# Four-layer graph network, layers 1-3: where the transposed adjacency matrix comes from

## The chip, the cores and the metric

The kernel runs on one core of one Trainium2 chip, in float32 throughout. The metric is the device time of one launch in microseconds (us). PE is TensorE, DVE is VectorE, ACT is ScalarE, POOL is GpSimd, and SP is the engine whose queue issues most of the DMA transfers.

## The reference, cut to what matters

There are 64 graphs (B) of 256 nodes (N) with 256 features (D). Each of the four layers is x = layernorm(x + layer(x, adj)). adj is a non-negative weighted matrix of each graph with a random pattern of zeros; the pattern is symmetric but the weights are not, so that the transpose is a different matrix.

- Layer 0 is a recurrence over the 256 nodes (a gated unit whose input is a row of adj's transpose times the states so far).
- Layer 1 is a normalized graph convolution:
```
degree = sum(adj, -1);  dis = where(isinf(degree ** -0.5), 0, degree ** -0.5)
out = relu((adj * dis[:, :, None] * dis[:, None, :]) @ (x @ W.T + b))
```
- Layer 2 is single-head attention with relu'd q, k, v; its scores are multiplied by adj and shifted by -9e15 * (1 - adj), then softmax, then a product with v and an output product.
- Layer 3 is attention with 8 heads of 32 features, masked where adj is not above 0:
```
scores = where(adj > 0, q @ k.T / sqrt(32), -9e15);  attn = softmax(scores);  out = (attn @ v) @ Wo + bo
```

## The kernel before, in words

`_recurrence` does layer 0 for all graphs, one node after another, until about 1527 us of the profiled execution. It leaves its result Hd in device memory. `_layers` (L911) then does layers 1, 2 and 3, and the last function runs only if a flag on the softmax's range is raised.

In `_layers` each graph is an object of class `Graph` (L1021) whose methods each emit one step. The order is written out by hand: `ROUND` (L1245) lists the steps of one round, and the loop at L1256 goes through the rounds. The letter ahead of a step says which graph it works for: in round t, L is graph t+1, A is t, B is t-1, C is t-2 and E is t-3. So five graphs are in work at once, at different stages, and a graph passes through five rounds. Each engine executes its instructions in the order in which this list emits them (the schedule is manual), and waits where an operand isn't there. The last line of `ROUND` holds the step that the change touches, `L.adT`, and `B.norm_a.2`; ahead of it stand `C.s3.1` and `B.f2`; the next round begins with `A.xT.1 B.xT.2 E.o3`.

The steps that matter here:

- `load` (L1029), at the head of round t for graph t+2: three DMAs of 256 KB on SP's queue, x, adj (tile `ad`, in natural layout, 128 rows by two halves) and y, layer 0's result. Within SP's queue they stand in that order; y's load of the first graph waits for layer 0's last store.
- `degrees_a`, `degrees_b` (L1049): row sums of `ad`, and dis by a power on POOL.
- `adT` (L1064): `flipped` (L981) takes a PSUM bank and transposes `ad` with four 128x128 PE instructions (L986, shown as tr_ad). ACT copies the two halves to SBUF with the factor dis (L1068, tile `adT`), and DVE makes layer 3's mask `neg3` from the same bank (L1073): -9e15 where the transposed entry is not above 0, else 0. `adT` is read by the step `g` of layer 1 one round later, `neg3` by the two `s3` steps three rounds later.
- `xT` (L1075): the same four PE transposes for y (tr_x), and one ACT copy (L1078). `xT.1` feeds `t`, `xT.2` feeds layer 2's `qk2`, `xT.3` feeds layer 3's.
- `product` (L991): a 256x256x256 product into a PSUM bank, L996 for all of them; the name of the bank tells which (mm_2f, mm_t, ...; plain mm are the q and k products).
- `s3` (L1170): for four heads, transposed scores on PE (L1180), the mask added on DVE (L1189, tile p), exp on ACT (L1190), and the sum of p's two halves on POOL (L1192, tile p3s).
- `o3` (L1196): sums over p3s by a product with ones on PE (L1206), and the heads' outputs (L1215); `sums(1)` comes last. It reads what `s3.0` and `s3.1` of the round before made.
- `f2` (L1140): the end of layer 2: DVE scales the product mm_2f by the softmax sums (L1144, two halves, tile f) and adds it to y with a relu (L1148).
- `norm_a`, `norm_b`: layernorm's statistics on DVE (L948 to L951), a power on POOL (L952), the shift on DVE (L958) and the scaling on ACT (L960).
- `masks` (L1095): layer 2's shift from `ad` on POOL (L1097).

The PSUM banks `mm` are four, used in turn by every `flipped` and `product`. Tiles of `new` have two buffers unless a number is given, `neg3` has four, `ad` has four, `y` seven.

Of the kernel before, what the change touches and what calls it, by code (L numbers as in the profile page):

```python
# [9 lines left out]
F32 = mybir.dt.float32  # L10
BF16 = mybir.dt.bfloat16
AF = mybir.ActivationFunctionType
ALU = mybir.AluOpType
AX = mybir.AxisListType

NEG = 9000000000000000.0
# [3 lines left out]
P = 128  # L20
# [890 lines left out]
def _layers(tc, ident, Hd, Yd, x, adj, weights, out):  # L911
# [8 lines left out]
    nc = tc.nc  # L920
# [7 lines left out]
    with ExitStack() as ctx:  # L928
# [9 lines left out]
        io = ctx.enter_context(tc.tile_pool(name="l_io", bufs=3))  # L938
# [26 lines left out]
        def bank(name, shape=(P, 2, D)):  # L965
            return ps.tile(list(shape), F32, tag="mm", name=name, bufs=4)

        for c in range(2):
            pt = bank(f"w1_{c}", (P, 2, P))
# [11 lines left out]
        def flipped(src, t):  # L981

            pt = bank(f"tr_{t}")
            for a in range(2):
                for c in range(2):
                    nc.tensor.transpose(  # L986
                        pt[:, a, c * P:(c + 1) * P], src[:, c, a * P:(a + 1) * P], ident
                    )
            return pt
# [12 lines left out]
        def new(tag, t, bufs=2, shape=(P, 2, D)):  # L1002
            return work.tile(list(shape), F32, tag=tag, name=f"{tag}_{t}", bufs=bufs)
# [17 lines left out]
        class Graph:  # L1021
# [7 lines left out]
            def load(self):  # L1029
                b = self.b  # L1030
                self.xin = io.tile([P, 2, D], F32, tag="xin", name=f"xin_{b}")
                nc.sync.dma_start(self.xin, x[b].rearrange("(c p) d -> p c d", p=P))
                self.ad = io.tile([P, 2, N], F32, tag="ad", name=f"ad_{b}", bufs=4)
                nc.sync.dma_start(self.ad, adj[b].rearrange("(c p) m -> p c m", p=P))
                self.y = io.tile([P, 2, D], F32, tag="y", name=f"y_{b}", bufs=7)
                nc.sync.dma_start(self.y, Hd[:, b, :].rearrange("(c p) d -> p c d", p=P))

# [24 lines left out]
                nc.vector.tensor_mul(self.dis, self.dis, self.some)  # L1062

            def adT(self):  # L1064
                pt = flipped(self.ad, f"ad_{self.b}")
                self.adT_sb = new("adT", self.b)
                for c in range(2):
                    nc.scalar.activation(  # L1068
                        self.adT_sb[:, c, :], pt[:, c, :], AF.Copy, scale=self.dis[:, c:c + 1]
                    )  # L1070

                self.neg3 = new("neg3", self.b, 4)
                nc.vector.tensor_scalar(self.neg3, pt, 0.0, -NEG, ALU.is_le, ALU.mult)  # L1073

            def xT(self, l):  # L1075
                pt = flipped(self.y, f"x{l}_{self.b}")
# [179 lines left out]
        for t in range(-1, B + 3):  # L1256
            if 0 <= t + 2 < B:
                graphs[t + 2].load()
            for step in ROUND:
                who, name, *args = step.split(".")  # L1260
                b = t - "LABCE".index(who) + 1
# [213 lines left out]
```

## Time and profile before

| | |
|---|---|
| median of three runs | 3438.73 us (3435.99 to 3442.99) |
| span of the profiled execution | 3437.6 us |
| layer 0, to the last of its PE work | about 1525.7 us |
| layers 1-3, from there | about 1912 us |
| one steady round (tr_ad at 2010.71, then 2039.58) | 28.85 us |
| busy over the span, PE | 3227.2 us (94%) |
| busy over the span, DVE | 2499.7 us (73%) |
| busy over the span, ACT | 1883.7 us (55%) |
| busy over the span, POOL | 1873.5 us (55%) |
| tr_ad on PE (L986), 128x128 | 273 ns each, four in 0.44 us |
| adT on ACT (L1068), 128x256 | 467 ns each |
| neg3 on DVE (L1073), 128x512 | 692 ns |
| layer 2's mask on POOL (L1097), 128x512 | 621 ns |

A row of the profile names the line, the engine, the operation and the tiles (what is written, then what is read), with their shapes. In a timeline, the first number is the start in us from the span's start, the second the time until the end of the group, and the square bracket the idle time ahead of it with the engine and line that ended it. The chain of waits goes back from the last instruction and shows, in order of time, which instruction stood on the path that set the end. The list of waits adds up, for each pair, how long an instruction's engine stood idle for another's result. Busy time of PE is modelled from the starts of pipelined matmuls, so that a busy PE isn't necessarily a PE at its peak.

### The profile page before, as it was taken

How to read it: one execution, taken by the hardware profiler on the slowest of the kernel's cores; microseconds unless marked ns; L12 is line 12 of the kernel's file. 1: busy time of each engine (PE TensorE's matmuls, PEld its weight loads, DVE VectorE, ACT ScalarE, POOL GpSimd, SP SyncE). 2: the span in 40 equal slices, each digit the busy share in tenths (PEclk: the TensorE clock that was granted, in tenths of full speed). 3: DMA queues.
4: the chain of work that ended last, by engine and by line, in shares of the span. 5: the costliest groups of instructions: out<-in, count | busy, mean ns of one | idle time of the engine just before them, and what ended most of it. 6: DMA issues, size and time to landing. Idle time of an engine off the chain costs nothing.

```text
span 3437.6 us, 80347 instructions
## 1 busy us (share of the span) xinstructions
PE 3227.2 (94%) x29350; PEld 2321.8 (68%) x29350; DVE 2499.7 (73%) x7061; ACT 1883.7 (55%) x5010; POOL 1873.5 (55%) x2165
## 2 busy tenths in 40 slices
PE   5699999999889998878999999999999999999997
PEld 3555555555455555547888888888888888888885
DVE  3377777766667777755888888888888887888775
ACT  0155555544445554535666666666666666666664
POOL 2376777766657777733444444444444444444443
PEclk8999999999999999988999999999999999999999
DMA  9856576788777575130111111111111111111100
GB/s 280 245 156 150 159 189 154 169 193 204 194 185 175 148 176 153 58 97 22 47 47 47 47 47 47 47 47 47 47 47 47 47 47 47 47 47 47 47 29 19
DMA packets 389348, 347.88 MB, mean 101 GB/s; under 512 B 107357, under 2 KB 355305, under 8 KB 383721
## 3 DMA queue, kind: packets, MB, share of 16 engines
q1 hardware_dynamic: 371256, 325.82, 35.4%
q10 hardware_dynamic: 17696, 16.91, 1.5%
q8 instruction: 234, 3.83, 0.5%
q14 instruction: 162, 1.32, 0.1%
HBM read 224.01 MB, written 99.61 MB: 94 GB/s over the span
## 4 chain that ended last, share of the span: by engine, by line
PE 73%; DMA 7%; DVE 7%; POOL 4%; issue 3%; ACT 3%; SPq 2%; ACTq 0%; DVEq 0%; POOLq 0%
PE mm L996 13%; PE rc L604 5%; PE s L1180 4%; PE rc L596 4%; PE mm_2f L996 3%; PE mm_3v L996 3%; PE mm_t L996 3%; PE mm_3f L996 3%; PE mm_2v L996 3%; PE mm_g L996 3%; PE mm_2s L996 3%; PE mm_2w L996 3%; PE o L1215 3%; PE late L520 3%; DVE ACC L629 3%
## 5 line engine op out<-in xcount | busy, mean ns | idle before, releaser
L629 DVE SCALAR_TENSOR_TENSOR ACC<-keep,S,ACC 128x128 f32<-128x128 f32 x1712 | 504.0, 344 | 186.4 <-ACT hs L647 171.5
L1192 POOL TENSOR_TENSOR p3s<-p 128x256 f32<-128x256 f32 x512 | 387.2, 788 | 369.1 <-ACT p L1190 369.0
L996 PE MATMUL mm<-xT,weights 128*128 128x256 f32 x2048 | 483.9, 385 | 3.2 <-ACT xT L1078 3.2
L996 PEld LDWEIGHTS mm<-xT,weights 128*128 128x128 f32 x2048 | 386.4, 191 | 80.6 <-issue 25.5
L1189 DVE TENSOR_TENSOR p<-s,neg 128x512 f32<-128x512 f32 x512 | 317.5, 682 | 118.2 <-PE s L1180 118.2
L666 POOL TENSOR_TENSOR ACC<-ACC,far 128x384 f32<-128x384 f32 (+1 forms) x313 | 372.7, 1191 | 24.5
L596 PE MATMUL rc<-WxT,xqT 128*64 128x256 f32 x2048 | 324.6, 396 | 3.7 <-ACT rc L837 1.2
L662 POOL TENSOR_TENSOR far<-hs,S 128x384 f32<-128x384 f32 (+1 forms) x313 | 304.9, 974 | 4.7
L960 ACT ACTIVATE y<-y,shift,rstd 128x256 f32<-128x256 f32 x512 | 273.4, 599 | 47.4 <-DVE shift L958 43.4
L1190 ACT ACTIVATE p<-p 128x512 f32<-128x512 f32 x512 | 295.2, 628 | 2.1 <-DVE p L1189 1.6
L803 POOL TENSOR_TENSOR ready<-ACC,dinv 128x128 f32<-128x128 f32 x255 | 102.3, 401 | 335.3 <-DVE ACC L629 335.2
L1103 ACT ACTIVATE qk<-mm,weights 128x256 f32<-128x256 f32 x256 | 107.5, 471 | 268.0 <-PE mm L996 268.0
L1092 POOL TENSOR_TENSOR y<-y,g 128x512 f32<-128x512 f32 x64 | 81.1, 1267 | 267.7 <-issue 267.7
L1229 DVE RECIPROCAL rT<-o 128x256 f32<-128x256 f32 x128 | 223.8, 1748 | 0.3 <-PE o L1206 0.2
L948 DVE BATCH_NORM_STATS2 st<-y 128x6 f32<-128x256 f32 x512 | 209.0, 408 | 13.5 <-POOL y L1092 12.7
L952 POOL TENSOR_TENSOR rstd<-rstd,mhalf 128x2 f32<-128x2 f32 x256 | 173.9, 698 | 82.1 <-DVE rstd L951 80.3
L613 ACT COPY xpT<-xpT_ps 128x128 f32<-128x128 f32 x256 | 68.3, 267 | 259.3 <-PE xpT_ps L611 259.3
L604 PE MATMUL rc<-WhT,xpT 128*64 128x128 f32 x2048 | 170.2, 288 | 29.1 <-ACT xpT L613 28.9
L1057 POOL TENSOR_TENSOR dis<-dis,mhalf 128x2 f32<-128x2 f32 x64 | 44.9, 702 | 276.0 <-DVE dis L1056 265.0
L604 PEld LDWEIGHTS rc<-WhT,xpT 128*64 128x64 f32 x2048 | 107.8, 137 | 120.2 <-ACT xpT L613 84.0
L1155 ACT ACTIVATE qk<-mm,weights 128x256 f32<-128x256 f32 x256 | 107.5, 471 | 118.4 <-PE mm L996 118.4
L596 PE MATMUL z_ps<-WxT,xqT 128*64 128x128 f32 x2048 | 169.7, 287 | 0.0
(162 smaller groups left out, 7418.4 us busy)
## 6 DMA issues: line engine op xcount, KB each, us to landing
xX<-in_x_dram ACTq DMA_DIRECT2D x16, 1024.0 KB
Us<-xu SPq DMA_DIRECT2D x64, 256.0 KB
xq<-in_x_dram SPq DMA_DIRECT2D x64, 256.0 KB
ACC<-Us SPq DMA_DIRECT2D x32, 512.0 KB
Es<-eu SPq DMA_DIRECT2D x64, 256.0 KB
early_sb<-Es SPq DMA_DIRECT2D x32, 512.0 KB
xin<-in_x_dram SPq DMA_DIRECT2D x64, 256.0 KB
ad<-in_adj_dram SPq DMA_DIRECT2D x64, 256.0 KB
```

What stands on the lines that cost most here:

```text
L596: nc.tensor.matmul(G[o * B:(o + 1) * B], xqT[a, i // 2][:, i % 2, kc, h * B:(h + 1) * B], WxT[:, kc, o, gates], start=False, stop=False, s ...
L604: nc.tensor.matmul(G[o * B:(o + 1) * B], hT[:, kc * B:(kc + 1) * B], WhT[:, kc, o, g], start=False, stop=(kc == 1), skip_group_check=True,)
L629: nc.vector.scalar_tensor_tensor(acc[:, 0, :], keep[:, j % 2, :], s, acc[:, 0, :], ALU.mult, ALU.add)
L662: nc.gpsimd.tensor_mul(tmp[:, 0:count, :], hs.unsqueeze(1).to_broadcast(shape), s.unsqueeze(2).to_broadcast(shape),)
L666: nc.gpsimd.tensor_add(acc, acc, tmp[:, 0:count, :])
L948: nc.vector.bn_stats(st, y[:, c, :])
L960: nc.scalar.activation(y[:, c, :], y[:, c, :], AF.Identity, bias=shift[:, c:c + 1], scale=rstd[:, c:c + 1],)
L996: nc.tensor.matmul(pm[:, c, :], lhsT[:, k, c * P:(c + 1) * P], rhs[:, k, :], start=(k == 0), stop=(k == 1),)
L1189: nc.vector.tensor_add(p, s_ps[i], self.neg3)
L1190: nc.scalar.activation(p, p, AF.Exp, scale=ISQ)
L1192: nc.gpsimd.tensor_add(both, p[:, 0, :], p[:, 1, :])
L1229: nc.vector.reciprocal(rT, o_ps[:, 1, :])
```

## The change

`load` gets a second load of adj, tile `az`, in eight DMAs between those of `ad` and y: each takes 32 columns of adj, all 256 rows, as eight blocks of 32x32, so that a row of a block is a run of 128 bytes. After them, partition j*32 + r of `az` holds row r of the blocks whose transposes belong on partitions j*32 to j*32 + 31 of adj's transpose, one block beside the other. `adT` turns all of these blocks by one DVE instruction, a transpose within 32x32 blocks over 128x512 elements, into a new SBUF tile `adTr`. PE's four transposes, and the PSUM bank that they took, are gone. ACT's scaled copies read `adTr` instead of the bank, and the mask `neg3` is made from `adTr` by POOL instead of DVE. The order in `ROUND` is the same. The steps `xT` and `pT2` still transpose on PE.

```diff
@@ load
                 nc.sync.dma_start(self.ad, adj[b].rearrange("(c p) m -> p c m", p=P))
+                self.az = io.tile([P, 2, 8, 32], F32, tag="az", name=f"az_{b}", bufs=3)
+                for j in range(4):
+                    for a in range(2):
+                        at = a * P + j * 32
+                        nc.sync.dma_start(
+                            self.az[j * 32:(j + 1) * 32, a],
+                            adj[b, :, at:at + 32].rearrange("(i r) c -> r i c", r=32),
+                        )
                 self.y = io.tile([P, 2, D], F32, tag="y", name=f"y_{b}", bufs=7)
@@ adT
-                pt = flipped(self.ad, f"ad_{self.b}")
+
+                turned = new("adTr", self.b)
+                nc.vector.transpose(
+                    turned.rearrange("p a m -> p (a m)"), self.az.rearrange("p a i c -> p (a i c)")
+                )
                 self.adT_sb = new("adT", self.b)
                 for c in range(2):
                     nc.scalar.activation(
-                        self.adT_sb[:, c, :], pt[:, c, :], AF.Copy, scale=self.dis[:, c:c + 1]
+                        self.adT_sb[:, c, :], turned[:, c, :], AF.Copy, scale=self.dis[:, c:c + 1]
                     )
 
                 self.neg3 = new("neg3", self.b, 4)
-                nc.vector.tensor_scalar(self.neg3, pt, 0.0, -NEG, ALU.is_le, ALU.mult)
+                nc.gpsimd.tensor_scalar(self.neg3, turned, 0.0, -NEG, ALU.is_le, ALU.mult)
```

Eight lines are added in `load` and three in `adT`, so that the lines of the changed kernel after `load` stand 8 to 12 higher.

## The prediction

> **What bounds the kernel now.** I read first the page's head and the busy time by stretch of the span, to see which part the change can touch.
>
> ```profile
> span 3437.6 us, 80347 instructions
> 1900.00:2300.00 400.00, 400.00 (x2693) 323.75 (x2693) 321.89 (x791) 254.76 (x554) 189.87 (x235) 1.00 0.14 45
> ```
>
> The second line gives busy us of PE, PE's weight loads, DVE, ACT and POOL, then clock and DMA share. From about 1530 us on, layers 1-3 run round after round, and PE is never idle. It looks as if every PE microsecond removed were a microsecond won. So I went to the chain of waits of one round (start, us, what), where the removed transposes stand:
>
> ```profile
> 2008.79 1.92 PE mm_2f L996 x8
> 2010.71 0.44 PE tr_ad L986 x4
> 2011.15 0.87 PE tr_x L986 x8
> 2012.02 0.57 PE o L1206 x8
> 2012.59 1.73 PE o L1215 x32
> 2014.32 0.92 PE o L1206 x8
> 2015.24 1.92 PE mm L996 x8
> ```
>
> tr_ad is 0.44 us of a 28.84 us round (tr_ad recurs at 2039.58). But the two groups of eight L1206 matmuls, the same work, take 0.57 and 0.92 us. The list of waits (total us, times, longest, over 2000 to 3200) names the rest:
>
> ```profile
> PEld o L1206 <- POOL p3s L1192: 14.5, 42, 0.6
> DVE p L1189 <- PE s L1180: 73.6, 42, 2.1
> DVE neg L1073 <- ACT adT L1068: 9.3, 42, 0.9
> ```
>
> 14.5/42 = 0.35 us a round: the second L1206 group waits for POOL's last p3s. Here PE is not the bound: the chain s (PE) to p (DVE) to exp (ACT) to p3s (POOL) is. Next, the DVE and ACT timelines of that stretch (start, duration):
>
> ```profile
> 2008.80 2.48 DVE L1189 TENSOR_TENSOR p<-s,neg 128x512 f32<-128x512 f32 x4 [1.74 <-PE s L1180]
> 2011.21 0.86 DVE L1144 SCALAR_TENSOR_TENSOR f<-mm_2f,sums,weights 128x256 f32<-128x256 f32 x2
> 2012.10 1.16 DVE L1148 SCALAR_TENSOR_TENSOR y<-f,y 128x512 f32<-128x512 f32 x1
> 2013.46 0.69 DVE L1073 TENSOR_SCALAR neg<-tr_ad 128x512 f32<-128x512 f32 x1 [0.20 <-ACT adT L1068]
> 2014.07 0.42 DVE L948 BATCH_NORM_STATS2 st<-y 128x6 f32<-128x256 f32 x1
> ```
> ```profile
> 2010.52 2.19 ACT L1190 ACTIVATE p<-p 128x512 f32<-128x512 f32 x4
> 2012.61 0.82 ACT L1068 ACTIVATE adT<-tr_ad,dis 128x256 f32<-128x256 f32 x2
> 2013.32 1.07 ACT L1078 COPY xT<-tr_x 128x512 f32<-128x512 f32 x2
> ```
> ```profile
> 2011.29 3.28 POOL L1192 TENSOR_TENSOR p3s<-p 128x256 f32<-128x256 f32 x4 [2.93 <-ACT p L1190]
> 2015.51 0.70 POOL L952 TENSOR_TENSOR rstd<-rstd,mhalf 128x2 f32<-128x2 f32 x1 [0.95 <-DVE rstd L951]
> 2015.17 1.99 PE L996 MATMUL mm<-xT,weights 128*128 128x256 f32 x8
> ```
>
> POOL's last p3s ends at 2014.57. ACT's second xT copy, which the mm at 2015.17 reads, ends at 2014.39: 0.78 us early. ACT could start adT at 2012.61 because tr_ad was done at 2011.15. DVE runs without a gap from 2008.80, when PE's scores release it, to the end of y at 2013.26.
>
> **What the Trainium skill says.**
> - "VectorE: DVE Perf Modes", The three transpose paths: DVE transposes 32x32 blocks only, and a 128x128 bf16 tile takes 311 ns. No transpose on DVE is in this trace.
> - "ScalarE: Activation LUTs", What ACT_TABLE_LOAD costs: an ACTIVATE takes 186 ns + 0.833 ns an element, 93 ns more for each [128,1] operand, and consecutive ones overlap by 93 ns. The trace agrees for SBUF sources (p, 512 elements: 613 by the page, 628 here; L960, 256 and two operands: 586, 599 here) and is quicker from PSUM (adT: 493, 467 here).
> - "SBUF — State Buffer", Who interferes with whom: a DVE instruction with two SBUF inputs or in a two-port mode and one of GpSimd exclude each other. Here y (L1148, two SBUF inputs) takes 1.16 us beside p3s, and 0.69 us at 1582.98 with POOL idle.
>
> **Removed.** Four transposes (0.44 us of PE) and a PSUM bank use per graph, 64 x 0.44 = 28 us of PE work. In the steady round they lie between the scores' end and the second L1206 group, which waits for POOL in any case: with tr_ad gone that wait is 0.35 + 0.44 us. I take a gain of nothing; the most it could be is 28 us. DVE's neg3, 0.69 us, goes too. It delays only norm_a, whose rstd POOL takes at 2015.51; nothing on PE waits for that.
>
> **Moved to POOL.** neg3 from SBUF: the same form at L1097 takes 0.62 us. It stands after the fourth p3s (2014.57) and ahead of rstd (2015.51), in POOL's 0.95 us of idle time, and layer 3 reads it rounds later: nothing. If it came late, rstd, then C.norm_b.2, would slip; these have more time if PE's round gets longer.
>
> **Added on DVE: the transpose, and its place.** In program order it stands behind both f and y, and ACT's adT now waits for it, while both xT copies are queued behind adT on ACT. That turns an idle cover into a path: PE scores, DVE p, f, y, transpose, ACT adT, xT, PE mm. The duration isn't in the trace. By the page's 311 ns for 128 elements at 0.96 GHz, 171 cycles are fixed, so 512 elements give (512 + 171)/0.96 = 711 ns: an estimate. Lower bound 0.68 us (the SBUF-read reduction of 128x512, L1052, 676 ns). Upper bound 1.3 us, if it needs two cycles an element (1.24 us) or must wait for p3s as y does (y's 1.16 - 0.69 = 0.47 us on top gives 1.2). I take 0.71. Its eight DMA waits become queue instructions of the kind seen ahead of L1148, 21 ns each; that one ran 1.3 us before its instruction started, so they hide behind y.
>
> **adT from SBUF.** One pointer operand, SBUF source: L1017 shows 502 ns, against 467 from PSUM. Two with 0.1 us overlap: 0.79 us until xT starts, instead of 0.71.
>
> The sum for a round, on the old clock: DVE instructions overlap by 0.08, so the transpose starts at 2013.18 and ends at 2013.89; ACT follows 0.03 later (as neg did after adT), 2013.92; xT starts at 2014.71, its pair takes 1.07: 2015.78; PE follows 0.06 later (as at 1542.07 after xT's end at 1542.01): 2015.84. Before: 2015.17. So **+0.67 us a round**, with everything after the mm unchanged, since DVE and POOL are early relative to it. With 0.68 for the transpose it is +0.64; with 1.3, +1.26.
>
> Graphs 4 to 63 pass through this steady round: 60 x 0.67 = 40 us. Graph 2 (y ends at 1583.67, mm at 1584.61): 1583.67 + 2.58 = 1586.25, +1.6, and PE's idle time there grows to some 3 us, after which matmuls ran at half speed elsewhere in the start-up; I take +2.5. Graph 3: y ends about 4.46 us after DVE's release at 1605.38, so mm at 1612.4 instead of 1611.26: +1.2. Graphs 0 and 1: nothing, adT waits there for ACT's own L960.
>
> **Added on SP: eight DMAs of 32 KB a graph**, 256 runs of 128 bytes each. Issue spacing is 0.51 us in SP's timeline (1530.62, 1531.13, 1531.63), so 4.1 us a graph, with y's load behind them. In steady rounds SP is idle from 2011.6 to 2019.3 and y is read a round later: nothing. The queue's mean packet takes 35.4% x 16 x 3437.6 / 371256 = 52 ns, so 2048 packets over 16 engines are 6.7 us at most a round of 28.8, at a DMA share of 14%. At the start it counts: y of graph 0 is issued at 1530.20 and POOL waits for it until 1533.90; eight issues ahead of it, 0.8 us of them in SP's present idle time, give +3.3, up to +6 if the packets are the limit. I take +4.
>
> **Sum:** 40 + 2.5 + 1.2 + 4 = 48 us on the span of 3437.6: 3485.6. The median of the runs, 3438.73, is 1.1 above the span: **3487 us**, +1.4%.
>
> **Rivals.**
> - *The transpose is slow or locks against POOL* (1.2 to 1.3 us). For it: POOL runs p3s at that very time, and DVE's two-input y suffers. Against: a transpose has one input. 60 x 1.25 = 75, with the start-up 83 or so: 3522.
> - *PE is the bound after all, faster.* The removed 0.44 us is won in 64 rounds: 3439 - 28 = 3411. It decides if xT is done by 2014.73 and the fourth p3s by 2014.1. Against: p3s ends at 2014.57 and its chain holds no removed instruction; the transpose can't start before DVE's f and y.
> - *Nothing moves:* the freed PE time is lost to POOL's wait, and ACT's queue is late by less than its 0.78 us of room; with the start-up 3443. It needs the transpose to end before 2013.2, so DVE would have to do it in no time.
> - *The PE clock drops,* or short packets choke the queue. PE's new idle time is about 0.75 us ahead of the mm; a gap of 1.02 us (before 1584.61) left it at full speed, one of 2.32 us (before 3399.81) did not, and matmuls took 2.93 us for six. That would add 2 us a round: 3600.
>
> **Chances.** The forecast 0.72 (its own range 3474 to 3503: transpose 0.60 to 0.85, start-up 5 to 12); slow transpose 0.14; clock or packets 0.05; nothing 0.05; faster 0.04. About 0.2% (7 us) can be told from no change: slower 0.91, same 0.05, faster 0.04. The range goes from the forecast's low end to just above the slow transpose: 3472 to 3526.
>
> **What would show it.** The round should be 29.5 us long; ACT's adT should wait for DVE's transpose, PE's mm L996 for ACT's xT by name, and the L1206 wait for POOL should grow to 0.8 us. The transpose's row should show 0.7 us. If rounds stay at 28.8, the queue argument on ACT is wrong; if they fall to 28.4, the POOL chain was no bound.

## The result, and the profile after

| | median of four runs (lowest to highest) | ratio to before, 95% interval |
|---|---|---|
| before | 3437.36 us (3435.08 to 3442.99) | |
| after | 3484.18 us (3480.14 to 3488.78) | 1.0123 (1.0107 to 1.0139) |

The changed kernel is slower by 1.2%, or 37 to 48 us by the interval. (The ratio is estimated from all runs and isn't the quotient of the two medians, which differ by 46.8 us.) The profiled execution of it has a span of 3487.0 us. The prediction for the median was 3487 us.

The page's head and the busy time by stretch, after (columns as before: PE, PE's weight loads, DVE, ACT, POOL, then clock, DMA share, GB/s):

```profile
span 3487.0 us, 80474 instructions
1900.00:2300.00 400.00, 391.07 (x2600) 313.23 (x2599) 321.43 (x776) 251.15 (x545) 212.22 (x244) 1.00 0.19 52
```

In the same 400 us PE, which had no gap before, is now idle for 8.9 us and issues 2600 matmuls, where it issued 2693. Its clock is still 1.00. The DMA share rose from 0.14 to 0.19: that is the second load of adj. A steady round, measured from one store of a result to the next (the median over the graphs), is 29.47 us instead of 28.85.

The chain of waits through the place of the change, after (start, us, engine and what):

```profile
2004.87 1.88 DVE p L1201 x3
2006.75 0.79 DVE f L1156 x2
...
2008.59 0.71 DVE adTr L1075
2009.32 0.91 ACT adT L1080 x2
2010.23 0.96 ACT xT L1090 x2
2011.23 1.99 PE mm L996 x8
```

Before, this stretch of the chain lay on PE alone (tr_ad, tr_x, o, mm). Now it leaves PE after the scores, runs through DVE's p, f, y (between the second and the third line) and the transpose, over to ACT's adT and xT, and comes back to PE's mm. PE's timeline shows the same from the other side (start, time to the end of the group, idle time ahead of it and who ended it):

```profile
2006.97 0.64 PE L1218 MATMUL o<-p3s,ones 128*32 128x256 f32 x8
...
2009.16 1.47 PE L1218 MATMUL o<-p3s,ones 128*32 128x256 f32 x8
2011.23 1.99 PE L996 MATMUL mm<-xT,weights 128*128 128x256 f32 x8 [0.61 <-ACT xT L1090]
```

Before, the second of the two groups and the mm behind it stood so:

```profile
2014.13 1.11 PE L1206 MATMUL o<-p3s,ones 128*32 128x256 f32 x8
2015.17 1.99 PE L996 MATMUL mm<-xT,weights 128*128 128x256 f32 x8
```

The two groups of sums are the same work; after the change the second takes 0.83 us longer than the first, because it waits inside for POOL's last p3s. After that wait there is a new one of 0.61 us, for ACT. From the start of this group to the start of mm it is 1.04 us before and 2.07 us after. Over the rounds between 1900 and 3000 us the medians are 1.02 and 2.08 us, and every other distance on PE's timeline is the same in both kernels: the growth of 1.06 us, less the 0.44 us of tr_ad, is the round's 0.62. The list of waits (total us, times, longest; 2000 to 3200):

```profile
ACT adT L1080 <- DVE adTr L1075: 49.8, 41, 1.2
...
PE mm L996 <- ACT xT L1090: 25.3, 41, 0.6
PEld o L1218 <- POOL p3s L1204: 22.6, 41, 0.6
```

The first two weren't there before: 49.8/41 = 1.21 us a round for ACT, and 25.3/41 = 0.62 us a round for PE. That this equals the growth of the round is a coincidence, since tr_ad went and the wait for POOL grew as well; E1 below takes the parts asunder. The third line grew from 0.35 to 22.6/41 = 0.55 us, where 0.8 was forecast. It counts only the idle time of the weight loads; by the length of the group the wait is longer (E3).

The rows of the new instructions (duration in ns: shortest/median/longest, then first and last start), and POOL's timeline behind p3s:

```profile
L1080 ACT ACTIVATE adT<-adTr,dis x128: 491/494/510, 1554.4 to 3395.0; 128x256 f32<-128x256 f32 x128
L1075 DVE STREAM_TRANSPOSE adTr<-az x64: 696/698/711, 1553.5 to 3393.8; 128x512 f32<-128x512 f32 x64
L1085 POOL TENSOR_SCALAR neg<-adTr x64: 1926/1927/1928, 1554.3 to 3395.3; 128x512 f32<-128x512 f32 x64
```
```profile
2006.68 3.27 POOL L1204 TENSOR_TENSOR p3s<-p 128x256 f32<-128x256 f32 x4 [2.90 <-ACT p L1202]
2010.03 1.93 POOL L1085 TENSOR_SCALAR neg<-adTr 128x512 f32<-128x512 f32 x1
2012.04 0.71 POOL L952 TENSOR_TENSOR rstd<-rstd,mhalf 128x2 f32<-128x2 f32 x1
```

The transpose takes 698 ns and adT from SBUF 494. The mask on POOL takes 1927 ns, three times what was predicted, and rstd, for which POOL waited before, now stands ready behind it.

### The profile page after: what moved, and what is told of

Its sections match the earlier page's. It is cut to its first block, busy times and chain, and to the rows that moved or that the text cites. A ratio compares the mean times of both kernels' runs of the same rounds, so it can differ in the third digit from the quotient of the medians.

```text
span 3487.0 us, 80474 instructions
## 1 busy us (share of the span) xinstructions
PE 3227.7 (93%) x29094; PEld 2309.6 (66%) x29094; DVE 2532.2 (73%) x7061; ACT 1887.1 (54%) x5010; POOL 1996.1 (57%) x2229
## 4 chain that ended last, share of the span: by engine, by line
PE 60%; DVE 13%; ACT 8%; DMA 8%; issue 5%; POOL 3%; SPq 2%; DVEq 0%; ACTq 0%; POOLq 0%
PE mm L996 13%; PE rc L604 5%; PE rc L596 4%; PE mm_t L996 3%; PE mm_3f L996 3%; PE mm_2v L996 3%; DVE ACC L629 3%; PE mm_2s L996 3%; PE mm_g L996 3%; PE s L1192 3%; PE late L520 3%; DVE p L1201 3%; PE mm_3v L996 3%; PE mm_2w L996 2%; PE z_ps L604 2%
## 5 line engine op out<-in xcount | busy, mean ns | idle before, releaser
L604 PE MATMUL rc<-WhT,xpT 128*64 128x128 f32 x2048 | 171.0, 289 | 29.0 <-ACT xpT L613 28.7
```

Of the source, the lines that this page charges most:

```text
L604: nc.tensor.matmul(G[o * B:(o + 1) * B], hT[:, kc * B:(kc + 1) * B], WhT[:, kc, o, g], start=False, stop=(kc == 1), skip_group_check=True,)
```

## Experiments

The theory was the prediction's: the transpose behind f and y holds adT on ACT, and xT, queued behind adT, comes late to PE. The rivals for the 0.62 us a round were the second load of adj, the read from SBUF, and POOL, whose mask runs over. "Round" is again the distance between two stores.

| kernel | median us | ratio to before, 95% interval | round us | layers 1-3 in the trace, us |
|---|---|---|---|---|
| before (profiled) | | | 28.85 | 1910.9 |
| after | 3484.18 | 1.0123 (1.0107 to 1.0139) | 29.47 | 1947.8 |
| E1, adT behind xT | 3436.04 | 0.9980 (0.9969 to 0.9991) | 28.78 | 1903.8 |
| E2, transpose ahead of s3 | 3437.36 | 0.9985 (0.9975 to 0.9995) | 28.78 | 1903.6 |
| E3, E1 and the sums later | 3407.16 | 0.9898 (0.9875 to 0.9922) | 28.28 | 1872.6 |
| E4, before and the sums later | 3448.17 | 1.0024 (1.0015 to 1.0033) | 28.91 | 1911.6 |
| E5, before and the loads | 3447.38 | 1.0006 (0.9999 to 1.0014) | 28.85 | 1909.5 |
| E6, mask on DVE | 3481.35 | 1.0115 (1.0099 to 1.0132) | 29.47 | 1951.3 |
| E8, transpose twice | 3533.84 | 1.0264 (1.0245 to 1.0283) | 30.21 | 1996.5 |
| E9, mask in two passes | 3480.62 | 1.0114 (1.0092 to 1.0135) | 29.41 | 1945.3 |

Each ratio is to runs of the kernel before on the same chip (for after, those of the first table; medians 3443.38 us for E1, E2, E3 and E5, 3441.37 us for E4, E6, E8 and E9). Layers 1-3 are counted from the end of layer 0's last DVE instruction, 1526.7 us before, to the end of the span.

**E1: ACT's adT behind xT.** The whole step, the transpose with it, is emitted behind both xT copies of the next round.

```diff
-            A.xT.1 B.xT.2 E.o3 E.d3.0 ...
+            A.xT.1 B.xT.2 A.adT E.o3 E.d3.0 ...
...
-            L.adT B.norm_a.2
+            B.norm_a.2
```

> The changed kernel with one step moved: adT (transpose, ACT copies, mask) is emitted in the next round right behind the two xT steps, so that no xT copy is queued behind it on ACT. Theory (ACT's queue: xT waits behind adT, which waits for DVE's transpose behind f and y): the round falls from 29.47 us to that of the kernel before, 28.85 us, since POOL's p3s chain holds PE there; layers 1-3 take about 1912 us and the run about 3440. PE as the bound (the freed 0.44 us is won once the queue is clear): 28.4 us a round, 3411. DVE's or the DMA's load as the cause (the place of adT doesn't matter): 29.4 us a round, 3480.

Measured: round 28.78 us, 0.69 less than after. The loads, the transpose, the read from SBUF and the mask on POOL are all still there; only the order on the queues differs. PE's timeline of E1 (columns as above):

```profile
2015.38 1.46 PE L1218 MATMUL o<-p3s,ones 128*32 128x256 f32 x8
2016.77 1.99 PE L996 MATMUL mm<-xT,weights 128*128 128x256 f32 x8
```

and ACT's:

```profile
2014.23 1.06 ACT L1090 COPY xT<-tr_x 128x512 f32<-128x512 f32 x2
2017.26 0.91 ACT L1080 ACTIVATE adT<-adTr,dis 128x256 f32<-128x256 f32 x2 [1.97 <-DVE adTr L1075]
```

xT is done at 2015.29, long before mm, and the 0.61 us ahead of mm are gone. adT now waits even longer, 1.97 us, and what stands behind it on ACT has time (after adT, ACT waits another 0.64 us for PE's mm): a wait costs by what is queued after it. PE's first line is the other half: the group of sums still takes 1.46 us, so that the step from its start to mm is 1.39 us, where it was 1.04 before. Of the 0.44 us of tr_ad, 0.35 went into this wait for POOL (0.37 by the medians). The rival "PE is the bound", 28.4 us a round, falls with that. The 0.62 us of the changed kernel are thus a sum of three: -0.44 for tr_ad, +0.37 for the longer wait for POOL, and +0.69 for the late xT, which E1 takes away.

**E2: the transpose alone, earlier.** The DVE instruction becomes a step of its own ahead of `C.s3.1`; adT stays where it is on ACT.

```diff
-            def adT(self):
-                turned = new("adTr", self.b)
-                nc.vector.transpose(...)
+            def turn(self):
+                self.turned = new("adTr", self.b)
+                nc.vector.transpose(...)
+            def adT(self):
+                turned = self.turned
...
-            B.pT2 E.norm_b.3 E.store A.norm_b.1 C.s3.1 B.f2
+            B.pT2 E.norm_b.3 E.store A.norm_b.1 L.turn C.s3.1 B.f2
```

> The changed kernel with only DVE's transpose moved, into DVE's idle time ahead of the second group of p additions; ACT's copies and the mask stay in place. Theory: adT no longer waits for f and y, ACT goes on right after exp, xT is done about 0.6 us ahead of PE's need, POOL's p3s chain holds PE: 28.85 us a round, 3440. If the reading of adT from SBUF, the slow mask on POOL or the loads were the cost, the round would stay near 29.4.

Measured: 28.78 us again.

```profile
2008.41 0.70 DVE L1074 STREAM_TRANSPOSE adTr<-az 128x512 f32<-128x512 f32 x1
2010.25 2.49 DVE L1204 TENSOR_TENSOR p<-s,neg 128x512 f32<-128x512 f32 x4 [1.14 <-PE s L1195]
```

Here adT still stands ahead of xT and still reads from SBUF, so neither the read nor adT's place is what costs; it is that its input came late. DVE does the transpose in the gap in which it waits for PE's scores: the rest of that gap is 1.14 us, where the gap was 1.74 us before the change.

**E3: E1, and the second sums of layer 3 later.** To win the freed time, the product that waits for POOL has to leave its place: `sums(1)` becomes a step behind `B.qk2.0`.

```diff
-                sums(1)
+                self.sums = sums
+            def o3s(self):
+                self.sums(1)
...
-            A.xT.1 B.xT.2 E.o3 E.d3.0 B.qk2.0 C.norm_b.2 E.d3.1
+            A.xT.1 B.xT.2 A.adT E.o3 E.d3.0 B.qk2.0 E.o3s C.norm_b.2 E.d3.1
```

> As the run with adT behind xT, and in addition the second group of sums over p3s stands behind the first q product on PE, so that PE doesn't wait for POOL's last p3s. Theory (POOL's chain is what eats the freed PE time): the wait of 0.35 us and the 0.44 us of the transposes are both won, about 28.1 us a round, 61 rounds, about 3393. If the round stays at 28.85, something else than p3s holds PE.

Measured: 28.28 us, short of the 28.1 that was expected, and a median of 3407.16 us, 1.0% (0.8 to 1.25%) faster than before. This version beats both kernels. PE's timeline of E3:

```profile
2011.38 1.91 PE L1227 MATMUL o<-p,v 128*32 128x256 f32 x32
2013.22 2.00 PE L996 MATMUL mm<-xT,weights 128*128 128x256 f32 x8
2015.14 0.64 PE L1218 MATMUL o<-p3s,ones 128*32 128x256 f32 x8
2015.71 2.00 PE L996 MATMUL mm_t<-W1T,xT 128*128 128x256 f32 x8
2017.54 1.89 PE L996 MATMUL mm<-xT,weights 128*128 128x256 f32 x8
```

The sums take 0.57 us to the next start (2015.14 to 2015.71) instead of E1's 1.39, and no longer wait. Measured by this 0.57, the wait for POOL was 1.04 - 0.57 = 0.47 us before and is 0.82 us in E1. But some of the 0.82 us comes back. From start to start, mm takes 1.92 us (E1: 1.83), mm_t 1.83 (E1: 1.73), and the heads 1.84 us to the start of what follows (E1: 1.72). The heads' 0.12 us isn't a wait for xT: ACT's last copy ends at 2013.00, 0.22 us ahead of mm, and the weight loads' idle time there is 0.41 us, the same as E1's ahead of mm, where xT is long done. In E3 the products change three times between the 32-column and the full 128-column form in this stretch (heads to mm, mm to sums, sums to mm_t), in E1 once. 0.82 - 0.09 - 0.10 - 0.12 = 0.51 us, and the round is 0.50 us below E1's. So the two more changes cost 0.31 us together. The rest of the round agrees: in the traces of before, after, E1 to E4, E6 and E8 (1900 to 3000 us), a full product between two full ones takes 1.73 us from start to start, one with a group of another form on one side 1.82 to 1.84, and mm in E3, with 32-column groups on both sides, 1.92. What in the change of form costs this was not tried by itself.

**E4: the same in the kernel before.** Only `o3s` is moved, and PE keeps its transposes of adj.

> The kernel before, with PE's transposes of adj kept, and only the second group of sums over p3s put behind the first q product. Theory: the wait for POOL (0.35 us) goes, but xT, ready at 0.28 us after PE gets there, is next, so about 0.15 us a round are won: 28.7 us, about 3429. If the whole wait is won, 28.5 us and 3416.

Measured: 28.91 us and a ratio of 1.0024, slower where a gain was expected: a miss. PE's timeline of E4, and its wait for xT (total us, times, longest):

```profile
2018.96 1.91 PE L1215 MATMUL o<-p,v 128*32 128x256 f32 x32
2020.99 1.99 PE L996 MATMUL mm<-xT,weights 128*128 128x256 f32 x8
```
```profile
PEld mm L996 <- ACT xT L1078: 24.9, 41, 0.6
```

(The list counts the weight loads' idle time, of which 0.41 us are there in E1 and E3 too.) From the heads' start to mm's are 2.03 us, where 1.72 led to the sums: with the sums out of the way mm comes early, and in the kernel before ACT's adT stands ahead of xT there too, though its input is in time; xT ends at 2020.94. Of these 0.31 us, 0.12 are the change of form, as in E3, and 0.19 the wait for xT. With the 0.09 and 0.10 us by which mm and mm_t grow as in E3, they take more than the 0.47 us that the sums save (1.04 - 0.57). The expectation had a wait of 0.28 us for xT, and no price for mm and mm_t: that is the term that it lacked.

E3 and E4 differ on PE only in two places: tr_ad, 0.44 us, and the heads' stretch, 2.03 for 1.84 us. Together these are the 0.63 us between their rounds. So the transposes' 0.44 us are won once the sums have moved and ACT's queue is clear. The kernel before with both moves (adT behind xT, and the sums later) was not run; taking the 0.19 us off E4 gives an estimate of 28.7 us a round for it, so that most of E3's gain should be the transposes.

**E5: the second load alone**, in the kernel before; `az` is loaded and nobody reads it.

> The kernel before with the eight extra loads a graph, whose tile nobody reads. Theory: rounds unchanged at 28.85 us, 2 to 4 us at the start of layers 1-3 because y's first load stands behind eight more issues, so 3440 to 3442. If short packets slow layers 1-3 or layer 0, the round or layer 0 is longer: layer 0 ended 12.5 us later in the profiled run of the changed kernel than before, and if the loads were the reason for that, it shows here too.

Measured: the round is 28.85 us, as before, and the ratio 1.0006, with an interval that reaches 1 (the medians differ by 4.0 us). At the start it shows: POOL waits 11.03 us for the first y, where it waited 7.82 us. The time from layer 0's end to the first store grows by 1.4 us (107.95 to 109.35). The loads aren't the cause of the 0.62 us.

**E6: the mask on DVE.** `nc.gpsimd.tensor_scalar` for `neg3` becomes `nc.vector.tensor_scalar`, with the rest as after.

> The changed kernel with the mask neg3 on DVE again, made from the turned tile in SBUF; POOL's 1.93 us a graph go. Theory (the mask isn't on the path): the round stays at 29.47 us, 3480 to 3487. If POOL's slow mask was part of the loss, the round is shorter, towards 28.85.

Measured: 29.47 us, the same as after. POOL is free of the 1.93 us, and DVE has 0.91 us more behind the transpose. The list of waits still has PE's mm waiting for xT, 24.7 us in 40 times, as in the changed kernel (25.3 in 41), so that the two shifts don't just cancel each other: the mask isn't on the path on either engine.

**E8: the transpose twice.** A second, equal transpose into the same tile follows the first.

> The changed kernel with DVE's transpose done twice, the second over the first. Theory (the transpose lies on the path that sets the round, one for one): one more transpose less the overlap of 0.08 us, +0.62 us a round, 30.09 us, 60 rounds, +37 us: about 3521. If it had room, less.

Measured: 30.21 us, 0.74 us more, and 3533.84 us.

```profile
2020.20 0.70 DVE L1075 STREAM_TRANSPOSE adTr<-az 128x512 f32<-128x512 f32 x1
2020.93 0.71 DVE L1078 STREAM_TRANSPOSE adTr<-az 128x512 f32<-128x512 f32 x1
2023.60 2.00 PE L996 MATMUL mm<-xT,weights 128*128 128x256 f32 x8 [1.36 <-ACT xT L1093]
```

The two start 0.73 us apart: the overlap of 0.08 us that the expectation took off isn't there between them, which is most of its miss of 0.12 us. PE's idle time ahead of mm grows from 0.61 to 1.36 us, by 0.75. So what DVE takes longer at this place, the round takes longer. E1, E2 and E8 together show the cause: the transpose's place behind f and y, ahead of adT.

**E9: the mask as arithmetic, in two passes on POOL.** It tries whether the comparison makes the pass slow.

```diff
-                nc.gpsimd.tensor_scalar(self.neg3, turned, 0.0, -NEG, ALU.is_le, ALU.mult)
+                nc.gpsimd.tensor_scalar(self.neg3, turned, 1.0e30, 1.0, ALU.mult, ALU.min)
+                nc.gpsimd.tensor_scalar(self.neg3, self.neg3, -1.0, NEG, ALU.add, ALU.mult)
```

> The changed kernel with POOL's mask by two arithmetic passes (multiply and minimum, then add and multiply) instead of one with a comparison. The comparison pass took 1.93 us, the arithmetic one of layer 2's mask 0.62. If the operation is what costs, two passes take 1.24 us together; if it is the tile or the neighbours, they take 1.9 each. The round stays at 29.47 us, since the mask isn't on the path.

Measured, rows of the masks' tile in E9 (ns: shortest/median/longest; L1110 is layer 2's own mask, an addition and a multiplication):

```profile
L1085 POOL TENSOR_SCALAR neg<-adTr x64: 1922/1922/1925, 1547.8 to 3385.5; 128x512 f32<-128x512 f32 x64
L1086 POOL TENSOR_SCALAR neg<-neg x64: 617/617/619, 1549.8 to 3387.6; 128x512 f32<-128x512 f32 x64
L1110 POOL TENSOR_SCALAR neg<-ad x64: 617/617/618, 1567.6 to 3415.9; 128x512 f32<-128x512 f32 x64
```

The pass with `min` is as slow as the one with `is_le`; the pass with add and mult, which reads and writes the tile that the first has just written, is quick. It isn't the shape, then, nor the tile that is written, nor the neighbours, since the slow pass takes 1922 to 1925 ns in all 64 graphs, start and drain included. Two things are left that both slow passes have and both quick ones lack: a comparison or a minimum, and `adTr` as the tile that is read. No run parts the two, so that the cause stays open. POOL has 0.62 us more to do than after, and the round is no longer for it (29.41 us).

## Why the prediction was right, step by step

**The round: right.** +0.67 us was forecast, +0.62 measured. (tr_ad at 2010.71 and 2039.58 are 28.87 us apart, not 28.84 as the prediction has it; the median from store to store is 28.85.) The chain is the one that was drawn, instruction by instruction. The parts: transpose 0.70 us (forecast 0.71); adT 0.91 us for the pair, or 494 ns each (forecast 502); and y, 0.06 us shorter (1.10 for 1.16), the cause of which was not looked for. The 711 ns were an estimate: the figure of the Trainium skill, "VectorE: DVE Perf Modes", The three transpose paths, for another size and type, carried over to 512 float32 elements at one cycle an element. The trace's 698 ns agree with the estimate within 2%; at other sizes no run here tries it.

**tr_ad's 0.44 us, a gain of nothing: right to within 0.1 us.** In E1, where the new path is cleared, the round is still 28.78 us. The wait that took the gain was forecast to go from 0.35 to 0.79 us; by the length of the group it went from 0.47 to 0.82. The round isn't quite 28.85: the exps of the first four heads end 0.07 us earlier. Why they do was not settled.

**The start: too high.** Forecast +4 for the loads, +2.5 and +1.2 for graphs 2 and 3. The trace, counted from layer 0's end, shows y of graph 0 2.5 us later (POOL waits 10.34 us instead of 7.82), mm of graph 2 3.5 us later, and mm of graph 3 4.3 us later (88.9 us for 84.6): +4.3 instead of 7.7. PE's idle time ahead of graph 2's mm is 1.5 us longer (2.50 for 1.02), part of which is the place of its tr_ad, and the clock doesn't drop after it.

**The mask on POOL: the duration was wrong, the conclusion held.** I took 0.62 us from a row of the same shape and the same instruction, L1097, which adds and multiplies where the mask compares and multiplies. The mask takes 1.93 us, and overran the 0.95 us of POOL's idle time by one. Nothing came of it, as E6 shows, since what stands behind it on POOL (rstd, and then the sum for y) has time.

**The sum: nearer than its parts.** The medians differ by 46.8 us (by the ratio it is 42), the two profiled executions by 49.4 us, and the forecast was 48. The traces split the 49.4 so: layer 0 +12.5 (its end at 1526.7 and at 1539.2), start +4.3, rounds from graph 3's mm to the drain +36.5, drain -3.9. Layer 0 has the same instructions in both, and its end lies between 1526.7 and 1539.2 us in the ten traces of this study, in no order that follows the change (E4, without the loads: 1532.6; E1, with them: 1529.5). In these two traces its matmuls ran at a lower mean clock after (0.94 for 0.96 between 600 and 1100 us). In the drain 2.5 us are one group of sixteen matmuls that took 6.18 us before (mean granted clock 0.59 between 3406 and 3413.2 us) and 3.72 us after (1.00 between 3460 and 3464 us). Layers 1-3 grew by 36.9 us where 48 were forecast; that the median landed within 3 us of the number is partly chance. The four runs of the kernel before that stand beside it also have a lower median than the later ones of the same kernel (3437.36 for 3443.38 and 3441.37 us). Sign and mechanism aren't chance, nor is the growth of the round.

**The rivals.** The slow transpose fell with the row of 698 ns. The clock stayed at 1.00 with idle times of 0.61 us, and of 1.36 us in E8. The prediction misread where it had dropped before: the six matmuls that took 2.93 us in the kernel before stand behind a second gap, of 1.97 us (granted clock 0.50 between 3402.4 and 3406 us), while the two right behind the gap of 2.32 us took 0.70 us, as two of the same product do at 3423.59 us, in a stretch with the clock at 1.00; and the gap of 2.50 us at the start left the clock up. "Nothing moves" fell by the round. "PE is the bound" was nearest in E1 and E2, and still wrong by 0.4 us; tr_ad's 0.44 us counted only when the sums had moved too (E3 against E4).

## What to carry to other kernels

When a step moves to another engine, look at what stands behind its reader in the reader's queue: here an instruction with 0.78 us to spare was held up by 0.6 us more than that, and moving one word in the list of steps took all of it back. Time freed on a busy engine is won only if the next wait on it is also cleared; find that wait beforehand (here the sums that waited for POOL) and move its reader, and count what the new neighbours cost. Try the two clearances apart and together: here E1, with ACT's queue cleared in the changed kernel, gave 0.2%, E4, with the sums moved in the kernel before, lost 0.2%, and E3, the changed kernel with both, gave 1%.

## What had not been expected of the hardware

- A POOL tensor_scalar over 128x512 float32 took 1927 ns with is_le and mult, 1922 ns with mult and min (both read adTr), and 617 to 621 ns with add and mult (from other tiles). On DVE the is_le form took 692 ns from PSUM, and from adTr in SBUF 910 ns (median in E6; shortest 427).
- A group of full products next to a group of another form took about 0.1 us longer on each such side: 1.73 us from start to start between full ones, 1.82 to 1.84 with one such side, 1.92 with two (mm in E3 and E4).
- Layer 0, unchanged, ended anywhere within 12.5 us from one traced execution to the next. A difference of less than some 10 us between two traces of this kernel is read from the rounds and not from the span.
